# A graph layer's last 724 nodes: three closing chunks in place of two, the last one fetched right behind the last store, in whole tiles and PSUM banks of its own

## The chip, the cores and the metric

The program runs on one core of one Trainium2 chip. A core has TensorE (PE in the profile, with PEld for its weight loads), VectorE (DVE), ScalarE (ACT), GpSimd (POOL) and SyncE (SP, which here only issues transfers and loads registers). The metric is the device time of one execution in microseconds; several executions are timed and their median counts. Before the change the median of three runs is 1881.22 us (1880.9 to 1882.45).

## What is computed

One message-passing layer on a graph of 12,500 nodes with 64 features and 212,500 edges with 32 features, then a residual and a layer norm:

```python
msg_in = concat([nodes[row], nodes[col], edge_features])          # row = src, col = dst
messages = relu(msg_in @ mW1 + mb1) @ mW2 + mb2                   # 160 -> 128 -> 64
aggregated = segment_sum(messages, col, num_segments=12500)
upd = relu(concat([nodes, aggregated]) @ uW1 + ub1) @ uW2 + ub2   # 128 -> 128 -> 64
out = layernorm(x + upd)                                          # over the 64 features
```

The edges come sorted by `dst`, so the edges of a node lie together.

## The kernel before

**Groups of edges.** The edges are worked through in 554 groups (`G`) of 384 (`GE`, three tiles of 128; the last group has 148). For each edge of a group POOL fetches the 64 features of its source node by an indirect transfer, one instruction for each tile of 128 edges (`gather`, L193, into a ring `own_rows`). For some of the groups ahead of the last ten, ACT and DVE copy these features one column at a time from a transposed copy of x instead (`fetch`, L666 and L668). DVE writes beside the features a one-hot row of 32 places that tells which of the 32 nodes from the group's first node on the edge ends at (`onehot`, L430).

TensorE treats a group in three parts, each in a later step than the one ahead of it: `turn` (L456) transposes features and one-hot rows into PSUM, and ACT copies them to `own_operands` (L469); `hidden` (L482) multiplies them with weights in which 32 rows are the projected destination nodes (`own_wm`, loaded by SP at L420), and DVE applies the relu (L493); `sums` (L514) multiplies the one-hot rows with the hidden rows, which gives the sums of the hidden rows of 32 nodes and the number of their edges. ACT moves these (L469 or L524), and SP stores 64 rows of 129 numbers, the upper 32 of them zeros, at the group's first node in one of two tables in device memory (`by_node_177` and `by_node_178`, even and odd groups by turns; `store`, L445).

A step of the main loop over k is turn(k), hidden(k-3) and sums(k-6) up to k = 543. In the last ten steps (`SHORT`) it is turn(k), then one or two sums that are outstanding, then one or two hidden. Since all engines run their instructions in the order in which they are written, and a product waits for all that its step needs, TensorE falls behind wherever one of these is late.

**Updates of nodes.** When all edges of a chunk of 512 nodes (`CH`) are done, the chunk is updated. `plan` gives each chunk the first group that lies certainly behind it (`closes`). `step_update(g)` is called once after each sums(g); it starts a chunk `SETTLED` groups after `closes` when no other is under way, and otherwise does one of its twelve steps:

- `found` (L536): SP fetches the chunk's rows of both tables into two SBUF tiles. Their pool, `found_p`, has one buffer for each, and each fetch waits for the stores into its table.
- `counts`, `count_moved` (L546, L556): TensorE adds the two tables' edge numbers and turns them, by products with the identity matrix; ACT moves them out of PSUM.
- `all_sums`, `moved` (L546, L566): the same for the 128 sums, moved by DVE to `agg`.
- `inner`, `relu` (L572 to L574, L579): three products into one PSUM bank, from the sums, the edge numbers and x; ACT applies the relu.
- `outer`, `stats`, `root`, `scaled` (L586, L588, L595, L596, L602, L607, L610): for each tile of the chunk two products (residual and second layer), mean and variance, the root on ACT, the division, and one transfer of the output (L615).

All PSUM results of an update share one bank (`ups`, one buffer, named `u_ps`). The chunk of 512 nodes from 11,776 closes at group 546, so that it starts after sums(548) and its last steps come when all groups are done. The last chunk has 212 nodes, as two tiles of 106; it never closes, and starts when the chunk ahead of it is finished:

```python
while summed < G:
    step((sums, summed))
    summed += 1
    stored()
while now or waiting:
    step_update(G + SETTLED)
```

Of the kernel before, what the change touches and what calls it, by code (L numbers as in the profile page):

```python
# [10 lines left out]
F32 = mybir.dt.float32  # L11
# [9 lines left out]
P = 128  # L21
# [32 lines left out]
SETTLED = 2  # L54
# [80 lines left out]
def ordered(ctx: ExitStack, tc: tile.TileContext, a, own, ok):  # L135
# [393 lines left out]
    def update(base, p, n):  # L529

        rows, q = slice(base, base + p * n), p * n

        def found():
            parts = [found_p.tile([P, 4, ROW], F32, name=f"found{i}") for i in range(2)]
            for t, table in zip(parts, tables):
                nc.sync.dma_start(t[:p, :n], table[rows, :].rearrange("(n p) w -> p n w", p=p))  # L536
            return parts
# [4 lines left out]
        def joined(parts, w, rows_out):  # L542
            ps = ups.tile([H, CH], F32, name="u_ps")[:rows_out]
            for k in range(n):
                for i, t in enumerate(parts):
                    nc.tensor.matmul(ps[:, k * p : (k + 1) * p], t[:p, k, w], ident[:p, :p],  # L546
                                     start=i == 0, stop=i == 1)
            return ps

# [3 lines left out]
        def count_moved(got):  # L553
            parts, ps = got
            count = up.tile([1, CH], F32, name="count")
            nc.scalar.activation(count[:, :q], ps[:, :q], AF.Copy)  # L556
            return parts, count

        def all_sums(got):
            parts, count = got  # L560
            return joined(parts, slice(0, H), H), count

        def moved(got):
            ps, count = got
            agg = up.tile([H, CH], F32, name="agg")
            nc.vector.tensor_copy(agg[:, :q], ps[:, :q])  # L566
            return agg, count

        def inner(moved_to):
            agg, count = moved_to  # L570
            u_ps = ups.tile([H, CH], F32, name="u_ps")
            nc.tensor.matmul(u_ps[:, :q], wc, agg[:, :q], start=True, stop=False)  # L572
            nc.tensor.matmul(u_ps[:, :q], per_edge, count[:, :q], start=False, stop=False)  # L573
            nc.tensor.matmul(u_ps[:, :q], ux, xc[: D + 1, rows], start=False, stop=True)  # L574
            return u_ps

        def relu(u_ps):
            u = up.tile([H, CH], F32, name="u")
            nc.scalar.activation(u[:, :q], u_ps[:, :q], AF.Relu)  # L579
            return u  # L580

        def outer(u):
            y = ups.tile([H, CH], F32, name="u_ps")[:, : 4 * D].rearrange("p (n d) -> p n d", n=4)
            for k in range(n):
                at = k * p
                nc.tensor.matmul(y[:p, k], xc[: D + 1, base + at : base + at + p], same,  # L586
                                 start=True, stop=False)
                nc.tensor.matmul(y[:p, k], u[:, at : at + p], u2, start=False, stop=True)  # L588
            return y

        def stats(y):
            parts = up.tile([P, 4, nc.vector.BN_STATS_DIM], F32, name="stats")
            mv = up.tile([P, 4, nc.vector.BN_AGGR_DIM], F32, name="mv")
            for k in range(n):
                nc.vector.bn_stats(parts[:p, k], y[:p, k])  # L595
                nc.vector.bn_aggr(mv[:p, k], parts[:p, k])  # L596
            return y, mv

        def root(ym):
            y, mv = ym  # L600
            rstd = up.tile([P, 4], F32, name="rstd")
            nc.scalar.activation(rstd[:p, :n], mv[:p, :n, 1], AF.Sqrt, bias=eps[:p])  # L602
            return y, mv, rstd

        def scaled(ymr):
            y, mv, rstd = ymr
            nc.vector.reciprocal(rstd[:p, :n], rstd[:p, :n])  # L607
            o = up.tile([P, 4, D], F32, name="o")
            for k in range(n):
                nc.vector.tensor_scalar(  # L610
                    o[:p, k], y[:p, k], mv[:p, k, 0:1], rstd[:p, k : k + 1],
                    ALU.subtract, ALU.mult,
                )
            queue = nc.scalar if base + q == N else nc.sync
            queue.dma_start(out[rows, :].rearrange("(n p) d -> p n d", p=p), o[:p, :n])  # L615

        return [found, settled, counts, count_moved, all_sums, moved, inner, relu, outer, stats, root, scaled]
# [111 lines left out]
    waiting = [(closes, update(base, p, n)) for base, p, n, closes in PLAN]  # L729
# [466 lines left out]
```

## Time and profile before

| | |
|---|---|
| median of three timed runs | 1881.22 us |
| profiled execution, its own time | 1878.41 us |
| span of that execution on the core | 1876.7 us |
| POOL's last gather begins | 1833.38 us |
| the last group's store is issued | 1842.77 us |
| the last chunk's fetches are issued | 1851.94 and 1852.37 us |
| the output's last transfer is issued | 1871.30 us |

Times in the profile are counted from the start of the span. A row of the timeline has the start, the length, the engine (PEld is a weight load, SPq and ACTq are transfers issued by SP and ACT), the line, the operation, what it writes and reads, the shape, how many instructions are merged into the row, and in brackets the idle time of the engine ahead of it with what ended it. A product of 32-bit numbers shows as two MATMUL instructions, so x16 of a row are eight products. "PEclk" is the share of TensorE's full clock that was granted, and "DMA share" the mean busy share of the 16 transfer engines.

### The profile page before, as it was taken

The page shows a single profiled execution, that of the slowest core. Times are in us where ns is not written, and L with a number is a line of the kernel's source. Part 1 is how long each engine was busy: PE and PEld are TensorE (multiplying, and loading weights), DVE is VectorE, ACT ScalarE, POOL GpSimd, SP SyncE. Part 2 cuts the span into 40 slices and gives each one's busy share as a digit, 9 for nine tenths or more (in the row PEclk, how much of TensorE's full clock was granted, in tenths as well). Part 3 has the DMA queues.
Part 4 walks back from the last instruction along what each step waited for, and adds up shares of the span by engine and source line. Part 5 has one row for each costly group of instructions (what it writes and reads, how often), then busy time and mean ns, then how long its engine had stood idle before and what let it go on. Part 6 is the DMA issues. An engine that isn't in the chain of part 4 may idle for free. (4 is left out here: it accounts for less than half of the span.)

```text
span 1876.7 us, 66058 instructions
## 1 busy us (share of the span) xinstructions
PE 1495.1 (80%) x13157; PEld 1217.2 (65%) x13157; DVE 1362.5 (73%) x14069; ACT 1619.6 (86%) x13169; POOL 1385.6 (74%) x1473
## 2 busy tenths in 40 slices
PE   4777888888788778787787878878878878788785
PEld 4666666676676666666675666767656756666673
DVE  3346888888888887877777778778777777787731
ACT  3368999999999999999999999989999898999830
POOL 7777777777777777777777777777777777777770
PEclk9888999999999999999999989989989899999897
DMA  5544333333333333333333333333332323333330
GB/s 136 130 109 93 62 74 74 64 75 74 64 72 74 65 74 68 63 71 71 63 68 68 65 71 64 69 71 60 72 73 63 71 60 72 70 63 72 71 70 17
DMA packets 195851, 135.48 MB, mean 72 GB/s; under 512 B 61029, under 2 KB 170650, under 8 KB 195434
## 3 DMA queue, kind: packets, MB, share of 16 engines
q1 hardware_dynamic: 147678, 82.58, 19.0%
q0 software_dynamic: 46912, 48.10, 14.4%
q14 instruction: 307, 2.51, 0.5%
q8 instruction: 110, 1.80, 0.4%
q10 hardware_dynamic: 844, 0.48, 0.1%
HBM read 103.03 MB, written 27.95 MB: 70 GB/s over the span
## 5 line engine op out<-in xcount | busy, mean ns | idle before, releaser
L193 POOL DMA_INDIRECT own_rows<-in_x,src_sb x1466 | 1384.8, 945 | 447.9 <-issue 178.6
L668 ACT ACTIVATE own_operands<-own_xc 64x1 f32 x12480 | 1295.1, 189 | 28.4 <-issue 6.7
L666 DVE COPY own_operands<-own_xc 64x1 f32 x12480 | 893.7, 136 | 283.4 <-issue 177.5
L456 PE MATMUL own_ps<-own_ident,own_rows 128*96 128x128 f32 x1661 | 299.2, 292 | 302.6 <-ACT own_operands L668 109.6
L482 PE MATMUL own_pre<-own_wm,own_operands 128*128 128x128 f32 x3322 | 492.4, 288 | 0.0
L514 PE MATMUL own_ps<-own_h,own_rows 128*32 128x128 f32 x3322 | 482.3, 284 | 0.0
L456 PEld LDWEIGHTS own_ps<-own_ident,own_rows 128*96 128x96 f32 x1661 | 171.2, 132 | 424.7 <-ACT own_operands L668 205.4
L482 PEld LDWEIGHTS own_pre<-own_wm,own_operands 128*128 128x128 f32 x3322 | 444.3, 203 | 2.4 <-issue 1.6
L469 ACT ACTIVATE own_operands<-own_ps 96x513 f32<-96x513 f32 (+2 forms) x554 | 321.8, 581 | 129.5 <-PE own_ps L514 108.0
L493 DVE TENSOR_SCALAR own_h<-own_pre 128x384 f32<-128x384 f32 x553 | 300.1, 543 | 172.4 <-PE own_ps L514 134.7
L514 PEld LDWEIGHTS own_ps<-own_h,own_rows 128*32 128x32 f32 x3322 | 336.6, 116 | 6.0 <-issue 0.2
L514 PE MATMUL own_ps<-own_one,own_rows 128*32 128x1 f32 x3322 | 199.1, 175 | 3.2 <-ACT own_operands L469 1.7
L514 PEld LDWEIGHTS own_ps<-own_one,own_rows 128*32 128x32 f32 x3322 | 152.3, 114 | 75.3 <-issue 11.4
L430 DVE TENSOR_TENSOR own_rows<-iota,dlc 128x96 f32<-128x96 f32 x554 | 132.4, 240 | 0.0
L546 PE MATMUL u_ps<-own_ident,found 128*1 128x128 f32 (+2 forms) x784 | 110.6, 298 | 19.8 <-SPq L1155 11.2
L546 PEld LDWEIGHTS u_ps<-own_ident,found 128*1 128x1 f32 (+2 forms) x784 | 80.8, 144 | 39.4 <-issue 16.7
L397 PE MATMUL u_ps<-w1b,own_xc 65*128 65x128 f32 x196 | 34.8, 332 | 39.8 <-DMA own_xc<-in_xT 15.5
L397 PEld LDWEIGHTS u_ps<-w1b,own_xc 65*128 65x128 f32 x196 | 29.5, 230 | 45.6 <-issue 25.4
L400 ACT ACTIVATE t<-u_ps 128x512 f32<-128x512 f32 (+1 forms) x25 | 14.6, 586 | 41.1 <-DMA by_dst<-t 17.6
L586 PE MATMUL u_ps<-same,own_xc 65*128 65x64 f32 (+1 forms) x196 | 39.5, 283 | 1.1 <-ACT u L579 1.1
L588 PE MATMUL u_ps<-u,u 128*128 128x64 f32 (+1 forms) x196 | 38.3, 277 | 0.0
L586 PEld LDWEIGHTS u_ps<-same,own_xc 65*128 65x128 f32 (+1 forms) x196 | 29.9, 192 | 7.1 <-ACT own_operands L668 3.4
(69 smaller groups left out, 328.6 us busy)
## 6 DMA issues: line engine op xcount, KB each, us to landing
own_operands<-in_efT SPq DMA_DIRECT2D x138, 192.0 KB
own_rows<-in_x,src_sb POOLq DMA_INDIRECT x1466
by_node<-own_operands SPq DMA_DIRECT2D x554, 32.2 KB
found<-by_node SPq DMA_DIRECT2D x48, 258.0 KB
own_wm<-by_dst SPq DMA_DIRECT2D x554, 16.0 KB
by_dst<-t SPq DMA_DIRECT2D x24, 256.0 KB
out<-o SPq DMA_DIRECT2D x24, 128.0 KB
own_xc<-in_xT SPq DMA_DIRECT2D x12, 179.2 KB
```

Of the source, the lines that this page charges most:

```text
L193: nc.gpsimd.indirect_dma_start(out=s[:p, j, :D], out_offset=None, in_=x[:, :], in_offset=bass.IndirectOffsetOnAxis(ap=src_sb[:p, g * TG + ...
L397: nc.tensor.matmul(ps[:, j], xc[: D + 1, base + j * P :][:, :P], w1b, start=True, stop=True)
L430: places_by[g] = nc.vector.tensor_tensor(own.s[g % RING][:, :, D:], iota.unsqueeze(1).to_broadcast([P, TG, W]), dlc[:, g * TG : (g + 1) * ...
L456: nc.tensor.transpose(xt[:, j * P : j * P + p], sides[g] if g in sides and j == TG - 1 else s[:p, j, :], ident[:p, :p])
L469: after(nc.scalar.activation(t[r, c : c + n], ps[r, :n], AF.Copy), step))]
L482: nc.tensor.matmul(pre[:p, j, :], t[:, c + j * P : c + j * P + p], wm[g % NW], start=True, stop=True)
L493: relu_by[g] = [nc.vector.tensor_scalar(h, pre, 0.0, None, ALU.max)]
L514: did.append(nc.tensor.matmul(out_ps, s[:p, j, D:], of(j, p), start=j == 0, stop=j == len(sizes) - 1))
L546: nc.tensor.matmul(ps[:, k * p : (k + 1) * p], t[:p, k, w], ident[:p, :p], start=i == 0, stop=i == 1)
L586: nc.tensor.matmul(y[:p, k], xc[: D + 1, base + at : base + at + p], same, start=True, stop=False)
L666: by[engine] = nc.vector.tensor_copy(o, x_at)
L668: by[engine] = nc.scalar.activation(o, x_at, AF.Copy)
```

## The change

The plan has 26 chunks in place of 25: the 512 nodes from 11,776 become two chunks of 256 (from 11,776, closing at group 535, and from 12,032, closing at group 546), and the 212 nodes from 12,288 remain the last chunk. `SETTLED` is 1, so that each chunk starts one group earlier if nothing else is under way.

```diff
-SETTLED = 2
+SETTLED = 1
...
-    for e in [c * CH for c in range(1, N // CH + 1)] + [N]:
-        n = e - b
-        chunks.append((b, *((P, n // P) if n % P == 0 else (n // 2, 2)),
-                       next((g for g in range(G) if least(g) >= e), G)))
+    whole = N // CH * CH
+    for e in [*range(CH, whole, CH), whole - CH // 2, whole, N]:
+        chunks.append((b, e - b, next((g for g in range(G) if least(g) >= e), G)))
```

The last chunk is cut into a whole tile of 128 nodes and one of 84, and its sums are fetched for 256 nodes: the 44 rows behind the last node are set to zero at the start of the program, by four small transfers on SP.

```diff
+        for table in tables:
+            for n in range(N, NP, W):
+                m = min(W, NP - n)
+                nc.sync.dma_start(table[n : n + m, :],
+                                  own.st[0][D + W : D + W + m, GE : GE + ROW])
```

The last chunk's fetches stand right behind the last group's store, ahead of the steps that the chunk from 12,032 has left:

```diff
+    _, (find, *others) = waiting.pop()
+    parts = find()
     while now or waiting:
         step_update(G + SETTLED)
+    for other in others:
+        parts = other(parts)
```

It uses the four PSUM banks of the groups instead of the shared one, has its sums and edge numbers added in one step, and goes out in two transfers, one on ACT's queue and one on SP's. In every chunk `inner` now has x's product first and the sums' product last; in the last chunk x's product stands ahead of the moves.

```diff
+        def bank(i):
+            if final:
+                return (*own.pre, *own.ps)[i][:, :CH]
+            return ups.tile([H, CH], F32, name="u_ps")
...
+        def own_inner(ps):
+            nc.tensor.matmul(ps[:, :q], ux, xc[: D + 1, base : base + q], start=True, stop=False)
+            return ps
...
+        def both(parts):
+            ps = joined(parts, slice(0, H), 0)
+            count = joined(parts, slice(H, ROW), 1)
+            return parts, ps, count, own_inner(bank(2))
+
+        def both_moved(got):
+            parts, ps, count_ps, u_ps = got
+            agg, _ = moved((ps, None))
+            _, count = count_moved((parts, count_ps))
+            return agg, count, u_ps
...
+            if final:
+                for k, (p, queue) in enumerate(zip(sizes, (nc.scalar, nc.sync))):
+                    queue.dma_start(out[nodes[k], :], o[:p, k])
...
+        if final:
+            return [found, both, both_moved, inner, relu, outer, stats, root, scaled]
```

Three places show what moves. The first is SP's queue at the very end, from the store of group 550 on; `found` is a fetch, `out` an output. Before:

```order
L445 DMA by_node_177<-own_operands 64x516
L445 DMA by_node_178<-own_operands 64x516
L445 DMA by_node_177<-own_operands 64x516
L445 DMA by_node_178<-own_operands 64x516
L615 DMA out<-o 128x4x64
L536 DMA found_94544<-by_node_177 106x2x129
L536 DMA found_94545<-by_node_178 106x2x129
```

SP's queue at the same place after the change:

```order
L449 DMA by_node_177<-own_operands 64x516
L449 DMA by_node_178<-own_operands 64x516
L449 DMA by_node_177<-own_operands 64x516
L449 DMA by_node_178<-own_operands 64x516
L555 DMA found_94547<-by_node_177 128x2x129
L555 DMA found_94548<-by_node_178 128x2x129
L656 DMA out<-o 128x2x64
L653 DMA out<-o 84x64
```

The last chunk's fetches moved ahead of the output of the chunk before it, and an output of the last chunk is now on this queue.

The second place is TensorE from the transposition of the last group (the second row below is its tile of 20 edges) to the first product of the update behind it. Before:

```order
L456 MATMUL own_ps<-own_ident,own_rows 96x128
L456 MATMUL own_ps<-own_ident,own_rows 96x20
L514 MATMUL own_ps<-own_one,own_rows 32x1 x3
L514 MATMUL own_ps<-own_h,own_rows 32x128 x3
L546 MATMUL u_ps<-own_ident,found_94408 128x128
...
L482 MATMUL own_pre<-own_wm,own_operands 128x128
L482 MATMUL own_pre<-own_wm,own_operands 20x128
L514 MATMUL own_ps<-own_one,own_rows 32x1 x2
L514 MATMUL own_ps<-own_h,own_rows 32x128 x2
L572 MATMUL u_ps<-agg,wc 128x512
```

TensorE at the same place after the change:

```order
L460 MATMUL own_ps<-own_ident,own_rows 96x128
L460 MATMUL own_ps<-own_ident,own_rows 96x20
L518 MATMUL own_ps<-own_one,own_rows 32x1 x3
L518 MATMUL own_ps<-own_h,own_rows 32x128 x3
L486 MATMUL own_pre<-own_wm,own_operands 128x128
L486 MATMUL own_pre<-own_wm,own_operands 20x128
L518 MATMUL own_ps<-own_one,own_rows 32x1 x2
L518 MATMUL own_ps<-own_h,own_rows 32x128 x2
L566 MATMUL u_ps<-own_ident,found_94472 128x128
L566 MATMUL u_ps<-own_ident,found_94473 128x128
L566 MATMUL u_ps<-own_ident,found_94472 128x128
L566 MATMUL u_ps<-own_ident,found_94473 128x128
```

The eight products that add the sums of 512 nodes stood between the last group's transposition and its hidden rows; now four, for 256 nodes, stand behind the last group's sums.

The third place is TensorE in the first two of the last ten steps (turn, two sums, two hidden). Before:

```order
L456 MATMUL own_ps<-own_ident,own_rows 96x128 x3
L514 MATMUL own_ps<-own_one,own_rows 32x1 x3
L514 MATMUL own_ps<-own_h,own_rows 32x128 x3
L514 MATMUL own_ps<-own_one,own_rows 32x1 x3
L514 MATMUL own_ps<-own_h,own_rows 32x128 x3
L482 MATMUL own_pre<-own_wm,own_operands 128x128 x6
```

TensorE at the same place after the change:

```order
L460 MATMUL own_ps<-own_ident,own_rows 96x128 x3
L518 MATMUL own_ps<-own_one,own_rows 32x1 x3
L518 MATMUL own_ps<-own_h,own_rows 32x128 x3
L518 MATMUL own_ps<-own_one,own_rows 32x1 x3
L518 MATMUL own_ps<-own_h,own_rows 32x128 x3
L566 MATMUL u_ps<-own_ident,found_94229 1x128
L566 MATMUL u_ps<-own_ident,found_94230 1x128
L566 MATMUL u_ps<-own_ident,found_94229 1x128
L566 MATMUL u_ps<-own_ident,found_94230 1x128
L486 MATMUL own_pre<-own_wm,own_operands 128x128 x6
```

The edge numbers of the chunk from 11,776 are added in this step; its sums, its inner and its outer products follow in the next three steps, at the same spot.

More of the change, by code (lines that the diff above doesn't have):

```diff
@@ L527, in sums, with update, reads @@
         return did, [*relu_by[g], *copy_by[g], *([emptied] if emptied else [])], moved
-    def update(base, p, n):
-        rows, q = slice(base, base + p * n), p * n
+    def update(base, q):
+        final = base + q == N
+        n = (q + P - 1) // P
+        sizes = [min(P, q - k * P) for k in range(n)]
+        nodes = [slice(base + k * P, base + k * P + p) for k, p in enumerate(sizes)]
+        columns_of = [slice(k * P, k * P + p) for k, p in enumerate(sizes)]
+        def bank(i):
+            if final:
+                return (*own.pre, *own.ps)[i][:, :CH]
+            return ups.tile([H, CH], F32, name="u_ps")
+        def reads(i):
+            if final:
+                tc.declare_no_dep(i.ins, group="quiet", reason="TensorE's later product is waited for")
         def found():
@@ L560, in all_sums @@
             parts, count = got
-            return joined(parts, slice(0, H), H), count
+            return joined(parts, slice(0, H), 0), count
         def moved(got):
@@ L727, in row_fetch @@
             rows_by.setdefault(g, []).append(i)
-    waiting = [(closes, update(base, p, n)) for base, p, n, closes in PLAN]
+    waiting = [(closes, update(base, q)) for base, q, closes in PLAN]
     now = []
```

66 lines of the change are left out of this document (36 added, 30 removed).

## The prediction, made before the changed kernel was run

> **What bounds the kernel now.** I read the groups of POOL first, then the timeline from the last gather on, then the chain of waits, then windows of half a microsecond around the fetches.
>
> ```profile
> span 1876.7 us, 66058 instructions
> ...
> L193 POOL DMA_INDIRECT own_rows<-in_x,src_sb x1466 | 1384.8, 945 | 447.9 <-issue 178.6 <-DMA own_rows<-in_x,src_sb 132.3 <-ACT own_operands L668 92.3
> ...
> POOL own_rows L193 <- issue: 178.6, 586, 0.3
> POOL own_rows L193 <- DMA own_rows<-in_x,src_sb: 132.3, 434, 0.3
> ...
> 1833.38 0.90 POOL L193 DMA_INDIRECT own_rows<-in_x,src_sb  x1 [0.30 <-DMA own_rows<-in_x,src_sb]
> ```
>
> ACT is busiest by share, but POOL's 1466 gathers take 945 ns each with 447.9/1466 = 0.31 us between them, and no wait is longer than 0.3: 1466 x 1.25 = 1832 us, which is the span up to the last gather's end at 1834.28. POOL never stands still for another engine, so the stretch up to there is POOL's and **only the 42.4 us behind it can move**, unless the change makes POOL wait.
>
> ```profile
> 1838.18 2.05 PE L546 MATMUL u_ps<-own_ident,found 128*128 128x128 f32 x16
> 1840.07 0.71 PE L482 MATMUL own_pre<-own_wm,own_operands 128*128 128x128 f32 x4
> ...
> 1842.77 0.47 SPq L445 DMA_DIRECT2D by_node<-own_operands  x1
> 1851.43 0.40 SPq L615 DMA_DIRECT2D out<-o  x1
> ...
> 1852.37 0.69 SPq L536 DMA_DIRECT2D found<-by_node  x1
> ...
> 1859.91 1.22 PE L546 MATMUL u_ps<-own_ident,found 106*1 106x106 f32 x6 [2.11 <-SPq L1155]
> ...
> 1871.30 0.52 ACTq L615 DMA_DIRECT2D out<-o  x1
> ```
>
> From the last store (1842.77) the tail is: 9.6 us until the last chunk's second fetch is issued, behind the 512-node chunk's output; 7.5 us until it lands (1859.91); 11.4 us of the last chunk's own chain; 5.4 us from the last output to the end of the span.
>
> **Term 1, the last group.** TensorE now adds no sums ahead of the last group's hidden rows: 16 instructions, 1838.18 to 1839.96, go (-1.8). Against it the 256-node chunk from 11,776 now does its products in the last ten steps. By the rows above and below that is 8 of 16 instructions for the sums (0.9), as many for the numbers (0.9), three products of 256 columns at half of 1.05 (1.6) and half of the 16 from 1846.24 on (0.9): 4.3 us more. The second chunk's numbers are half as many (-0.9).
>
> ```profile
> 1804.08 0.51 PE L456 MATMUL own_ps<-own_ident,own_rows 128*96 128x128 f32 x3 [1.37 <-DMA own_rows<-in_x,src_sb]
> ...
> 1826.59 0.51 PE L456 MATMUL own_ps<-own_ident,own_rows 128*96 128x128 f32 x3 [0.47 <-DMA own_rows<-in_x,src_sb]
> ...
> 1830.38 0.50 PE L456 MATMUL own_ps<-own_ident,own_rows 128*96 128x128 f32 x3 [1.45 <-DMA own_rows<-in_x,src_sb]
> ```
>
> In these steps TensorE waits for gathered rows (the first row is where they begin), 0.5 + 1.5 us behind it. A TensorE that is late has no such waits, so they pay for 1.9 of the 4.3. Sum: 4.3 - 0.9 - 1.9 - 1.8 = **-0.3**, between -1.8 (all of the 4.3 hidden) and +1.6 (no wait pays). I take -0.2: the last store at 1842.6. What is queued behind TensorE there is ACT's move and that store, nothing else.
>
> **Term 2, the fetch.** It stands right behind the store. The first fetch waits until TensorE has read the second 256-node chunk's rows, for the buffer is the same: the last sums end 0.4 us ahead of the store's issue, and 8 instructions take 0.9, so about 1843.3. The second waits for the last store's landing.
>
> ```profile
> 1843.50:1844.50 1.00, 1.00 (x3) 0.24 (x3) 0.00 (x0) 0.00 (x0) 0.00 (x0) 1.00 0.14 33
> 1844.50:1845.50 1.00, 1.00 (x2) 0.22 (x2) 0.00 (x0) 0.00 (x0) 0.00 (x0) 1.00 0.00 0
> ...
> 1853.50:1859.30 5.80, 0.51 (x2) 0.12 (x2) 0.00 (x0) 0.00 (x0) 0.00 (x0) 0.50 0.14 39
> ...
> 1826.00:1829.20 3.20, 2.45 (x23) 1.79 (x21) 0.80 (x2) 0.76 (x2) 2.59 (x3) 1.00 0.80 197
> ```
>
> The last two numbers of a window are the DMA share and GB/s. The store issued at 1842.77 is over by 1844.5, 1.7 us: the second fetch is issued at 1844.4. The old fetch of 106 partitions crept at a share of 0.14, two engines of 16, for 5.8 us; the 128-partition fetch of the 512-node chunk ran at 0.80 and 197 GB/s. So 132 KB take 0.7 us in place of 2.9; with 1.3 us from issue to data (the store has none for 0.7 us, and is over after 1.7), it **lands at 1846.4**, within 1845.8 (data 0.7 behind the issue) and 1849.1 (132 KB still at 39 GB/s, 3.4 us). The Trainium skill ("DMA: Bandwidth & Descriptors", section "Why a DMA increments its semaphore by 16 and not by 1") has an HWDGE transfer use the largest number up to 16 that divides the slowest dimension: 2 engines for 106, 16 for 128. The trace agrees with the 2, and by the rule the 1849.1 falls away.
>
> **Term 3, the middle chunk.** On TensorE the second 256 nodes stand ahead of the last chunk's products.
>
> ```profile
> 1841.23 0.67 DVE L566 COPY agg<-u_ps 128x512 f32<-128x512 f32 x1
> 1843.38 1.12 PE L573 MATMUL u_ps<-count,per_edge 1*128 1x512 f32 x2
> 1844.43 1.12 PE L574 MATMUL u_ps<-own_xc,ux 65*128 65x512 f32 x2
> ...
> 1846.24 0.43 PE L586 MATMUL u_ps<-same,own_xc 65*128 65x64 f32 x2 [0.69 <-ACT u L579]
> ...
> 1847.85 0.39 PE L588 MATMUL u_ps<-u,u 128*128 128x64 f32 x2
> ```
>
> Its sums end at 1843.3; the move of 256 columns takes 0.45 (0.67 for 512 here, 0.39 for 212 in the chain below), three products 1.6, ACT's relu 0.45, four of these eight row pairs 0.9: with the handovers 1846.9. That is later than the landing, so the last chunk **starts at 1846.9** and the fetch has 0.5 us to spare.
>
> **Term 4, the last chunk's own chain.** Before:
>
> ```profile
> 1861.17 0.34 ACT count L556
> ...
> 1861.56 2.05 PE u_ps L546 x8
> 1863.64 0.39 DVE agg L566
> 1864.07 1.08 PE u_ps L572 x2
> 1865.14 1.00 PE u_ps L573 x2
> 1866.14 1.02 PE u_ps L574 x2
> 1867.18 0.35 ACT u L579
> ...
> 1869.32 0.24 DVE stats L595
> ...
> 1870.67 0.60 DVE o L610 x2
> ```
>
> TensorE ran at half its clock: 8 instructions in 2.05 us, 16 of the same form in 2.05 at 1838.18. After, at the full clock: sums 0.9, numbers 0.8, three products of 212 columns at 0.5 each, 1.5 (the moves by ACT and DVE lie beside the numbers and x's product; DVE first ends the middle chunk, 2.0 behind 1846.9 as below, its move is there at 1849.4, and the product that needs it comes at 1849.6), relu 0.45, six instead of eight outer instructions 0.8 (the first pair lies beside the relu), then as before 2.0 from `stats` to the output (1869.32 to 1871.30): 6.4. The output is issued at **1853.3**, 18.0 earlier than 1871.30.
>
> **Term 5, the way out.** The span ends 5.4 us behind the last output. That output now leaves by ACT and by SP, both over 16 or nearly 16 engines. But SP used to be long past its last branch.
>
> ```profile
> L1155 SPq EVENT_SEMAPHORE  x8: 17/17/17, 1856.5 to 1874.6; - x8
> L1155 SPq COMPARE_BRANCH  x1: 54/54/54, 1853.7 to 1853.7; - x1
> ```
>
> It branched at 1853.7 and went on at 1856.5, 2.8 us later. Now it issues (0.4), loads its flag (0.6, from the fetch's issue ending at 1853.06 to the branch), stands for 2.8, checks its eight semaphores (some 0.2), and needs what lies between the last of them and the end, 1874.6 to 1876.7 (2.1): 6.1 us. I take +0.8; below, -1.0 if only the faster landing counts, above +1.0.
>
> **Nothing** I charge for the rest. `SETTLED` shifts the updates by one group, and the four transfers of zeros delay SP's first loads by some 2 us (four issues of 0.5): both lie beside POOL, whose gathers run up to 16 groups (60 us) ahead; without that cover the 2 us would stay.
>
> **Sum:** -0.2 from the store, 1842.6 to 1853.3 in place of 1842.8 to 1871.3 (-17.8), +0.8: **-17.2**. The profiled execution took 1878.41 (span 1876.7 and 1.7 around it), 2.8 less than the median of the three runs, 1881.22; I take the difference from the median: 1864.0.
>
> **Rivals.** *The half clock comes back.*
>
> ```profile
> 1770.84 0.85 PE L456 MATMUL own_ps<-own_ident,own_rows 128*96 128x128 f32 x3 [2.40 <-DMA own_rows<-in_x,src_sb]
> ...
> 1804.00:1812.00 8.00, 7.34 (x78) 6.54 (x79) 1.67 (x4) 2.05 (x6) 6.03 (x7) 1.00 0.27 59
> ...
> 1770.00:1777.20 7.20, 6.36 (x38) 4.75 (x39) 3.78 (x41) 5.34 (x45) 5.37 (x6) 0.53 0.41 79
> ...
> 1848.50:1849.00 0.50, 0.00 (x0) 0.00 (x0) 0.43 (x5) 0.00 (x0) 0.00 (x0) 0.68 0.00 0
> ```
>
> A wait of 2.40 us left the granted clock at 0.53 for 7 us, while that of 1.37 ahead of 1804.08 left 1.00; at the tail it fell half a microsecond behind the last product. The new tail has pauses of 0.5 us only, but several, and short products between them. If it falls, the last chunk's products take twice their 3.8 us (0.9 + 0.8 + 1.5 + 0.6): 1867.8. The Trainium skill ("TensorE: Matmul & The Clock Gate", section "What's actually happening") lets the half rate return only after an idle window of about 3.4 us. By that there is no pause for this rival and the time is 1864.0; the trace differs, as 2.40 us sufficed. I give it 0.20.
>
> *The fetch isn't early.* It shares its buffers with the middle chunk. Were it held until that chunk's output, as now, the fetch would go out at about 1849.3 (1846.9, 2.0 from statistics to output, and 0.4 of its issue) instead of 1844.4; it would land at 1851.3, 4.4 later: 1868.4. Against it: the order has only the middle chunk's sums ahead. 0.07.
>
> *More is hidden:* term 1 at -1.8 and a way out of -0.2 instead of +0.8 give 1861.4. 0.08.
>
> *The tail gains, but something else ends last*, with no change of time: 1881. Nothing in the chain speaks for it. 0.04.
>
> *Slower: SP stands at each fetch.*
>
> ```profile
> SPq L536 <- DMA by_node<-own_operands: 24.3, 23, 2.4
> ```
>
> SP waits 1.06 us for each chunk's fetch until a store has landed. If with `SETTLED = 1` each of the 25 fetches in the loop waited for a store more, as long again, the loads of `own_wm` behind it would be late by 25 x 1.06 = 26 us; where POOL's lead of 16 groups is used up, that reaches the end: 1864.0 + 26 = 1890. It decides from 17.2/25 = 0.7 us a chunk. Against it: the fetch follows the newest store in both kernels, and POOL never waits. 0.03.
>
> **How the numbers follow.** The forecast, 1864.0 (1862 to 1866.2 by term 1's and the landing's bounds), has 0.58. To keep 8 in 10 the range takes in the clock's rival, the held fetch and the better case: 1860 to 1869. Faster by over 0.2% (3.8 us, about what a measurement of this kernel can tell from no change) are all but the last two: 0.93; same 0.04, slower 0.03.
>
> **What would show it.** Right: POOL's last gather still near 1833.4; the last store within 1.7 us of 1842.6; the last fetch about 1.8 us behind it; TensorE's last sums following the middle chunk's outer products without a wait; the last outputs near 1853; SP last at the barrier. Wrong: gaps above 0.3 us between gathers; a wait of over 1 us ahead of the last chunk's sums; a granted clock of 0.50 behind 1843; a last store beyond 1844.4.

## The result, and the profile after

| | before | after |
|---|---|---|
| median of six runs each | 1881.55 us (1879.58 to 1882.45) | 1868.09 us (1865.2 to 1869.99) |
| after / before | | 0.9927, 95% interval 0.9914 to 0.994 |
| profiled execution, its own time | 1878.41 | 1866.26 |
| span of that execution | 1876.7 | 1864.5 |

The kernel is 13.5 us faster by the medians (17.2 were predicted) and 12.2 us by the two profiled executions. The groups of the changed kernel have this for POOL (busy time and mean ns of one, then the idle time ahead of them and what ended it):

```profile
core 0 of [0], span 1864.5 us
...
L192 POOL DMA_INDIRECT own_rows<-in_x,src_sb x1466 | 1385.1, 945 | 447.8 <-issue 177.1 <-DMA own_rows<-in_x,src_sb 126.2 <-ACT own_operands L713 97.2
```

Its timeline, in part by engines:

```profile
1800.91 0.85 PE L460 MATMUL own_ps<-own_ident,own_rows 128*96 128x128 f32 x3 [2.23 <-DMA own_rows<-in_x,src_sb]
...
1833.56 0.89 POOL L192 DMA_INDIRECT own_rows<-in_x,src_sb  x1 [0.30 <-issue]
...
1844.79 1.16 PE L566 MATMUL u_ps<-own_ident,found 128*128 128x128 f32 x8
1845.24 0.47 SPq L449 DMA_DIRECT2D by_node<-own_operands  x1
1845.82 1.71 SPq L555 DMA_DIRECT2D found<-by_node  x2
1849.83 2.08 PE L566 MATMUL own_pre<-own_ident,found 128*128 128x128 f32 x16
1852.00 0.38 SPq L656 DMA_DIRECT2D out<-o  x1
1856.55 0.39 ACTq L653 DMA_DIRECT2D out<-o  x1
1856.80 0.39 SPq L653 DMA_DIRECT2D out<-o  x1
```

POOL is as it was: the same 0.31 us between gathers (447.8/1466), and the last begins 0.2 us later. The whole gain lies behind it. SP's fetch (L555) now follows the store directly, the last chunk's sums follow the middle chunk's products with no wait in brackets, and the last output goes out at 1856.80 instead of 1871.30. Of the 14.5 us gained there 2.3 are lost on the way out: 7.7 us to the end of the span, 5.4 before.

| us from the start of the span | predicted | measured |
|---|---|---|
| last store issued | 1842.6 | 1845.24 |
| last chunk's sums begin | 1846.9 | 1849.83 |
| last output issued | 1853.3 | 1856.80 |
| end of the span | 1859.5 | 1864.5 |

So 5.0 us less was gained in this execution than forecast: 2.6 up to the store, 0.3 in the middle chunk, 0.6 in the last chunk's chain (7.0 instead of 6.4) and 1.5 on the way out.

Two views of the changed kernel show where the first and the last of these arise. The windows (length, busy time of PE, PEld, DVE, ACT, POOL, granted clock, DMA share, GB/s):

```profile
1797.07:1800.48 3.41, 1.61 (x18) 1.22 (x17) 2.18 (x9) 0.74 (x2) 2.51 (x3) 1.00 0.53 110
1800.48:1810.72 10.24, 9.24 (x58) 7.08 (x59) 0.72 (x2) 1.62 (x4) 7.80 (x9) 0.50 0.34 77
...
1844.85:1848.27 3.42, 2.90 (x15) 1.79 (x14) 0.42 (x1) 0.27 (x1) 0.00 (x0) 1.00 0.29 48
1848.27:1851.68 3.41, 2.94 (x25) 2.45 (x24) 1.18 (x7) 0.68 (x2) 0.00 (x0) 1.00 0.16 43
```

TensorE had waited 2.23 us for gathered rows (the timeline's first row, the transposition of group 543, the last before the ten short steps), and from 1800.48 to 1810.72, in this step and the first short one, it ran at half clock. From there on it is the bound: no later step waits for rows. In the tail the clock was 1.00 in this execution. SP's instructions at the end of the program, in the list for their line (length of one in ns, first and last start):

```profile
L1204 SPq EVENT_SEMAPHORE  x8: 17/17/17, 1860.5 to 1862.8; - x8
...
L1204 SPq COMPARE_BRANCH  x1: 54/54/54, 1857.8 to 1857.8; - x1
```

And SP's waits behind 1844 (us in all, how many, the longest):

```profile
SPq L1204 <- SPq L1204: 4.4, 2, 2.6
```

SP branches at 1857.8, behind its output, stands 2.6 us, checks five of its eight semaphores, stands a further 1.8 (the other of the two waits) and is the last at the barrier.

### The profile page after: what moved, and what is told of

Same layout as the page of the kernel before. It is cut to its first block, busy times and chain, and to the rows that moved or that the text cites. A ratio compares the mean times of both kernels' runs of the same rounds, so it can differ in the third digit from the quotient of the medians.

```text
span 1864.5 us, 66091 instructions
## 1 busy us (share of the span) xinstructions
PE 1489.1 (80%) x13163; PEld 1213.9 (65%) x13163; DVE 1364.2 (73%) x14073; ACT 1619.0 (87%) x13172; POOL 1385.9 (74%) x1473
## 5 line engine op out<-in xcount | busy, mean ns | idle before, releaser
L192 POOL DMA_INDIRECT own_rows<-in_x,src_sb x1466 | 1385.1, 945 | 447.8 <-issue 177.1
L566 PE MATMUL u_ps<-own_ident,found 128*1 128x128 f32 (+1 forms) x768 | 103.4, 289 | 9.0 <-DMA found<-by_node 9.0
L566 PEld LDWEIGHTS u_ps<-own_ident,found 128*1 128x1 f32 (+1 forms) x768 | 76.7, 141 | 26.6 <-issue 7.5
L401 PE MATMUL u_ps<-w1b,own_xc 65*128 65x128 f32 x196 | 37.9, 353 | 36.3 <-DMA own_xc<-in_xT 17.2
L622 PE MATMUL u_ps<-same,own_xc 65*128 65x64 f32 x192 | 38.3, 281 | 0.5 <-ACT u L616 0.5
L623 PE MATMUL u_ps<-u,u 128*128 128x64 f32 x192 | 37.1, 275 | 0.0
L622 PEld LDWEIGHTS u_ps<-same,own_xc 65*128 65x128 f32 x192 | 29.0, 190 | 5.6 <-ACT own_operands L713 3.2
```

Of the source, the lines that this page charges most:

```text
L192: nc.gpsimd.indirect_dma_start(out=s[:p, j, :D], out_offset=None, in_=x[:, :], in_offset=bass.IndirectOffsetOnAxis(ap=src_sb[:p, g * TG + ...
L401: nc.tensor.matmul(ps[:, j], xc[: D + 1, base + j * P :][:, :P], w1b, start=True, stop=True)
L566: nc.tensor.matmul(ps[:, k * P : (k + 1) * P], t[:, k, w], ident, start=j == 0, stop=j == 1)
L622: nc.tensor.matmul(y[:p, k], xc[: D + 1, nodes[k]], same, start=True, stop=False)
```

## The experiments

All times below are compared with runs of the kernel before on the same chip. "Behind the gather" counts from the start of POOL's last gather in the same execution, since that varies by 2 us. An experiment's line numbers differ from the changed kernel's by up to 6.

### The changed kernel again, and parts of it undone

No edit; then one for each run:

```diff
 e2 and e4:
-                for k, (p, queue) in enumerate(zip(sizes, (nc.scalar, nc.sync))):
+                for k, (p, queue) in enumerate(zip(sizes, (nc.scalar, nc.scalar))):
 e3 and e4:
-    for e in [*range(CH, whole, CH), whole - CH // 2, whole, N]:
+    for e in [*range(CH, whole, CH), whole, N]:
```

> The changed kernel itself, once more, as the yardstick for the runs beside it. In its first profile the last store is issued 11.7 us behind the start of POOL's last gather (9.4 before the change), and TensorE ran at half its clock from 1800.5 to 1810.7 at the head of the last ten steps. If the lateness is the work of the added chunk, the 11.7 comes again, within 0.5. If it was the half clock, whose place is not the same in every execution, the store stands 9.4 to 10 us behind the gather where TensorE has its full clock there. The end of the span stands 7.7 us behind the last output; expected again, within 0.5. Time 1866 to 1870.

> Both outputs of the last chunk go by ACT's queue, SP has none. Theory: the way out is long because SP issues an output and only then branches to its end, 2.7 us, and stands a further 1.8 us before it goes on; without the output SP branches behind the middle chunk's output, early enough, and the end comes 5.4 to 6.2 us behind the last output instead of 7.7. The second issue on ACT costs 0.4, so 1.1 to 1.9 us less than the changed kernel. Rival: the end follows the landing of the last output, whoever issues it, or ACT branches just as late as SP did: no gain, up to 0.4 slower.

> The 512 nodes from 11,776 stay one chunk, all else as changed. Theory: the added chunk's products in the last ten steps are what makes the last store late, so it comes back to 9.4 us behind the last gather (11.7 with the split); the 512 nodes' outer products end as before the change, 14.9 us behind the gather, against 16.3 with the split, and the last chunk's sums start there. DVE is busier with four tiles of the chunk ahead and gives back up to 0.8: together 0.6 to 1.4 us less than the changed kernel. Rival, the split shortens the tail: the last chunk starts 1 to 2 us later than with it, because the products behind the last store are twice as many (16 instead of 8 for the sums, three products of 1.05 us each instead of 0.65).

> One chunk of 512 and both outputs on ACT's queue together. If both theories hold, the gains add: 1.7 to 3.3 us less than the changed kernel, near 1865.5. If only one of them holds, the gain is that of the single run within 0.5 us.

| | median of five | ratio to before (1881.17), interval | last store behind the gather | last sums to last output | last output to end |
|---|---|---|---|---|---|
| e1, changed again | 1868.61 | 0.993, 0.9917 to 0.9944 | 10.2 | 8.7 | 7.8 |
| e2, both on ACT | 1866.58 | 0.9919, 0.9905 to 0.9932 | 10.0 | 10.8 | 4.8 |
| e3, 512 as one | 1869.15 | 0.9932, 0.9919 to 0.9946 | 8.7 | 8.6 | 8.1 |
| e4, both edits | 1865.7 | 0.992, 0.9906 to 0.9933 | 8.6 | 7.7 | 4.7 |

**The way out is settled.** With no output of its own SP branches early, beside the last chunk's products, and its stand costs nothing. In e2's list for the same line:

```profile
L1204 SPq EVENT_SEMAPHORE  x8: 17/17/17, 1857.1 to 1865.2; - x8
...
L1204 SPq COMPARE_BRANCH  x1: 54/54/54, 1854.4 to 1854.4; - x1
...
L1204 ACTq COMPARE_BRANCH  x1: 58/58/58, 1863.4 to 1863.4; - x1
...
L1204 ACTq EVENT_SEMAPHORE  x1: 17/17/17, 1866.1 to 1866.1; - x1
```

The end comes 4.8 us behind the last output instead of 7.8, of which the second issue on ACT gives back 0.25. ACT does branch late, as the rival had it, and stands 2.7 us (1863.4 to 1866.1); what goes is what SP did behind that, a second stand of 1.8 us and its checks. So the rival (the landing decides, or ACT branches just as late, and nothing is gained) falls. The medians of e1 and e2 don't separate the two (their intervals overlap); the rows do: 7.7 to 8.4 us in the eight profiles of the changed kernel's variants in which SP has an output, 4.7 to 5.2 in the five in which it has none. A rule of the Trainium skill fits: a taken branch out of the instructions at hand forces a fetch of its target ("Runtime: NRT & Kernel Launch", section "Instruction fetch mechanics"); the stand behind the branch is there in both rows, from 1857.8 to 1860.5 in the changed kernel and from 1854.4 to 1857.1 here, but here the last chunk's products cover it.

**The yardstick was not steady.** e1 is the changed kernel, and its last chunk took 8.7 us instead of 7.0. Its windows:

```profile
1840.91:1844.33 3.42, 2.46 (x24) 1.60 (x23) 0.84 (x3) 0.82 (x3) 0.00 (x0) 1.00 0.08 19
1844.33:1847.74 3.41, 2.89 (x16) 1.84 (x16) 0.42 (x1) 0.27 (x1) 0.00 (x0) 1.00 0.22 46
1847.74:1851.15 3.41, 2.94 (x11) 2.22 (x12) 0.01 (x1) 0.38 (x1) 0.00 (x0) 0.50 0.17 46
1851.15:1854.57 3.42, 3.42 (x16) 2.31 (x15) 1.76 (x9) 0.30 (x1) 0.00 (x0) 0.50 0.08 19
```

The prediction's first rival, the half clock, is there in the tail. It came in e2 and e3 too and not in e4, which is why e3's time (expected 0.6 to 1.4 us below the changed kernel's, 0.5 above it) says nothing of the split. It also comes where no pause explains it. In the second row TensorE is busy for 2.89 of 3.41 us, and the next two stretches run at half clock; in the changed kernel's first profile 2.90 of 3.42 us (1844.85 to 1848.27) are followed by a full one. What may differ is how much the products in the stretch use of TensorE's 128 rows. Both have 1.25 us of light products, over 65 rows (x) and over one row (edge numbers); e1's has besides 0.3 us of products over 20 rows (the last group's last tile) where the other has as much over 128. With each product's time counted by its rows over 128, the stretch of e1 is busy for 0.50 of its time, that of the first profile for 0.58. e3, whose light products are longer, shows it best:

```profile
1840.66:1844.07 3.41, 2.84 (x13) 1.13 (x12) 0.48 (x2) 0.27 (x1) 0.00 (x0) 1.00 0.08 19
1844.07:1847.49 3.42, 2.73 (x4) 0.70 (x4) 0.00 (x0) 0.60 (x1) 0.00 (x0) 0.50 0.36 77
```

2.84 of 3.41 us are busy, by rows 0.33, and the clock falls. The Trainium skill's rule that the prediction cites ("TensorE: Matmul & The Clock Gate", section "What's actually happening": half rate after an idle window) would have kept the clock in e1 and in e3; the measurement decides. The count by rows isn't the whole of it: in e4 a stretch of 0.49 kept the full clock, and in e2 the one ahead of the half clock (1843.05 to 1846.46, busy for 2.53 us) has 0.56.

### The light products made heavy

The closing chunks' products over 1 and 65 rows are run over 128, with rows of zeros:

```diff
+    nc.vector.memset(xc[D:, 11776:N], 0.0)
...
-    ux = const.tile([D + 1, H], F32, name="ux")
-    per_edge = const.tile([1, H], F32, name="per_edge")
+    ux = const.tile([P, H], F32, name="ux")
+    per_edge = const.tile([P, H], F32, name="per_edge")
+    numbers = [const.tile([P, CH], F32, name=f"numbers{i}") for i in range(2)]
+    for t in (ux, per_edge, *numbers):
+        nc.vector.memset(t, 0.0)
...
+        rows, one = (P, P) if base >= 11776 else (D + 1, 1)
...
-            nc.tensor.matmul(ps[:, :q], ux, xc[: D + 1, base : base + q], start=True, stop=False)
+            nc.tensor.matmul(ps[:, :q], ux[:rows], xc[:rows, base : base + q], start=True, stop=False)
...
-            nc.tensor.matmul(u_ps[:, :q], per_edge, count[:, :q], start=False, stop=False)
+            nc.tensor.matmul(u_ps[:, :q], per_edge[:one], count[:one, :q], start=False, stop=False)
...
-                nc.tensor.matmul(y[:p, k], xc[: D + 1, nodes[k]], same, start=True, stop=False)
+                nc.tensor.matmul(y[:p, k], xc[:rows, nodes[k]], same[:rows], start=True, stop=False)
```

`same` is made 128 rows high likewise; the last two chunks' edge numbers go to one tile of `numbers` each. e6 adds the outputs on ACT, e7 the 512 nodes as one chunk. e8 is the changed kernel with this edit alone:

```diff
+FILL = 534
...
-            for j, p in enumerate(tiles_of(g))
+            for j, p in [*enumerate(tiles_of(g))] * (2 if FILL <= g < G - SHORT else 1)
```

> As changed, but in the closing chunks from node 11,776 on the products over 1 and over 65 rows (edge numbers and x) run over 128, the added rows being zeros; no more instructions in the tail, two or three small clearings at the start. Theory: the clock falls to half after a stretch of 3.4 us in which TensorE's busy time, each product counted by its rows of 128, stays below about 0.5; the tail's light products (1 and 65 rows) sink below that in about half of the executions, depending on where the stretches begin, and this costs 2 to 4 us. With 128 rows the tail keeps its full clock to the last products in this profile, the slow ones among the times (1868 to 1871) go, and the median is 1 to 3 us below the changed kernel's 1868.6, near 1866. Rival: rows don't count, only time in which TensorE does nothing; half clock in the tail as often as before, times 1865 to 1871, median within 0.5 of the changed kernel's.

> 128 rows and both outputs on ACT's queue. By the theory on rows the tail's clock stays full, by that on the way out the end comes 4.8 us behind the last output (7.8 with SP); together 2.5 us less than the run with 128 rows alone (3.0 for the way out, 0.5 given back for the second issue on ACT), near 1863.5. Rival: the gain of the output on ACT that the earlier run's median showed (2.0) is all of its clock's luck: within 0.5 of 128 rows alone.

> 128 rows, both outputs on ACT and the 512 nodes as one chunk. In the earlier run without the 128 rows, in an execution whose tail had its full clock, the last chunk's sums began 13.9 us behind the last gather, against 16.2 with the split. If that is what the split costs, this run is 2 us below the one beside it with the split, near 1861.5, with the last store 8.6 to 8.8 us behind the gather. Rival: the earlier start was the clock's alone at the head of the last ten steps; then both are equal within 0.5.

> As changed, but the groups 534 to 543 are transposed twice (three more transposes a step, 0.5 us, into the same place with the same result), so that TensorE waits less for gathered rows ahead of the last ten steps. Theory: in the profiles of the changed kernel a wait of 2.2 us there (busy share 0.43 to 0.47 of a stretch of 3.4 us) puts the first two or three of the last ten steps at half clock, and TensorE doesn't make that up again: with the wait filled the clock stays full and the last store stands 9.7 to 10.0 us behind the gather instead of 10.2 to 11.7; 0.5 to 1.7 us less time. Rival: the store is late by the added chunk's products alone; then it stays, and the transposes add up to 0.5 us.

These four ran on a chip that took 2634.29 us for the kernel before. Medians: e5 2625.83, e6 2624.5, e7 2615.26, e8 2630.21, single runs spread over 18 to 34 us. What bounds the kernel is another thing there, as e5's groups show:

```profile
L192 POOL DMA_INDIRECT own_rows<-in_x,src_sb x1466 | 1383.6, 944 | 1147.8 <-ACT own_operands L478 557.2 <-issue 297.1 <-ACT own_operands L719 258.6
...
L719 ACT ACTIVATE own_operands<-own_xc 64x1 f32 x12480 | 1352.2, 189 | 377.1 <-issue 354.7 <-DVE own_h L502 0.3
```

POOL waits 1147.8 us, mostly for ACT, and ACT stands 377 us between its column copies where it stood 28.5 in e1. The last store stands 64 to 70 us behind the gather, so the four times and the place of the store answer nothing, and e8's question, whether a filled wait at the head of the last ten steps brings the store forward, stays open. What the tails show from the last sums on can be used: in e5, e6 and e7 the last chunk ran at full clock, in e8, with the light products, at half; the way out is 7.7, 5.2, 5.1 and 7.8 us. The other questions were put again, with two more parts undone on top of the 128 rows: e10 issues the last chunk's fetches late, e11 gives it the steps and the shared bank of the other chunks. e9 is e5 and e12 is e7 once more.

```diff
 e10:
     _, (find, *others) = waiting.pop()
-    parts = find()
     while now or waiting:
         step_update(G + SETTLED)
+    parts = find()
 e11 (and bank and reads without their branch for the last chunk):
-            return [found, both, both_moved, inner, relu, outer, stats, root, scaled]
+            return [found, settled, counts, count_moved, all_sums, moved, inner, relu, outer, stats, root, scaled]
```

> The 128 rows alone once more, since the chip of the earlier run took 2634 us for the kernel before. As there: with the theory on rows the tail keeps its full clock up to the last products, the last chunk takes 6.8 us from its first sums to its last output, and the times of 1868 to 1871 go: median near 1866, 1 to 3 us below the changed kernel's 1868.6. Rival, only idle time counts: half clock in the tail as often as before, median within 0.5 of 1868.6.

> 128 rows, and the last chunk's fetches moved back behind the middle chunk's last step, as before the change. Theory: the early fetch carries the largest part of the gain that the new code on its own can have: the fetches go out behind the middle chunk's output, 7 to 7.5 us later than now; they land 2 to 3 us behind that, and the last chunk's sums, which follow the middle chunk's products without a wait now, wait 4 to 5 us. 4 to 5 us more than the run with 128 rows beside it. Besides, a wait of that length may put the last chunk at half clock: up to 7 more. Rival: the fetch is hidden either way, because TensorE is behind; less than 1 us.

> 128 rows, and the last chunk with the steps and the one PSUM bank of the other chunks: numbers, then sums, then the inner products, each behind the move of the one ahead; early fetch, whole tiles and the two output queues stay. Theory: its first product waits until DVE has read the middle chunk's rows out of the shared bank, 2.1 us behind that chunk's outer products, and each step adds a hand-over: 3.5 us more than the run with 128 rows beside it, 2.5 to 5, more if the pauses bring the half clock. Rival: the banks and the joint step don't matter, because DVE frees the bank in time: under 1 us.

> 128 rows, both outputs on ACT's queue and the 512 nodes as one chunk, once more: the candidate for the fastest. If the gains add: way out 4.8 to 5.2 us instead of 7.8 with a second issue of 0.5 on ACT (-2.3), last chunk's start 1 to 2 us earlier: 3 to 4.5 us less than 128 rows alone, near 1862. If one 512-node chunk only pays by its clock's luck: 2 to 2.5 less, near 1864.

| | median | ratio to before (1879.66), interval | last store behind the gather | store to last sums | last sums to last output | to end |
|---|---|---|---|---|---|---|
| e9, 128 rows | 1864.86 (1861.75 to 1866.08) | 0.9918, 0.9905 to 0.9932 | 11.4 | 4.2 | 6.8 | 7.9 |
| e10, late fetch | 1870.51 (1869.04 to 1871.44) | 0.995, 0.9936 to 0.9963 | 10.2 | 9.2 | 8.7 | 7.7 |
| e11, old chain | 1869.15 (1868.11 to 1871.11) | 0.9944, 0.993 to 0.9958 | 9.4 | 17.2 to the last output, together | | 8.4 |
| e12, 128 rows, ACT, 512 | 1861.52 (1860.95 to 1862.96) | 0.9903, 0.9887 to 0.9918 | 9.0 | 4.9 | 7.7 | 4.8 |

**The rows.** In e9 the tail keeps its full clock up to the last product, and no run reaches 1868 (the kernel before took 1.5 us less on this chip than on e1's). Its windows:

```profile
1844.42:1847.83 3.41, 2.87 (x16) 2.03 (x14) 0.42 (x1) 0.27 (x1) 0.00 (x0) 1.00 0.23 48
1847.83:1851.24 3.41, 2.96 (x25) 2.46 (x25) 1.35 (x7) 0.68 (x2) 0.00 (x0) 1.00 0.17 44
1851.24:1855.20 3.96, 2.43 (x15) 1.90 (x14) 1.15 (x8) 0.98 (x3) 0.00 (x0) 1.00 0.09 21
```

The first is e1's stretch again, busy for 2.87 us against 2.89, and this time the clock stays. Over all traces with an early fetch and banks of its own, the last chunk's products met half clock in four of six with the light products (e1, e2, e3, e8; not the first and e4) and in none of five with 128 rows (e5, e6, e7, e9, e12). It is no guarantee: in e7 the chunk ahead of the last one met half clock for 3.4 us, behind a stretch that was busy for 0.72 of its time, by rows 0.63. The expected 1 to 3 us are there by the medians as ratios, 0.9918 against e1's 0.993, but the intervals overlap and e1 ran on another chip, so the times alone don't exclude the rival (within 0.5 us); the clock in the traces speaks against it.

**The early fetch** is worth 5.65 us (1870.51 - 1864.86): in e10 TensorE waits 4.8 us for it, and the pause puts the chunk at half clock.

```profile
1850.90 0.92 SPq L561 DMA_DIRECT2D found<-by_node  x2
...
1853.21 4.04 PE L572 MATMUL own_pre<-own_ident,found 128*128 128x128 f32 x16 [4.82 <-DMA found<-by_node]
```

No run undoes the whole tiles alone, so their share stays open. **Banks of its own and the joint step** are worth 4.3 us (1869.15 - 1864.86), the half clock that comes without them included. In e11 the first product waits for DVE's last reading of the shared bank, the sums wait for the numbers' move, and from 1851.07 on it runs at half clock (the window below the timeline's rows):

```profile
1850.24 1.11 PE L570 MATMUL u_ps<-own_ident,found 128*1 128x128 f32 x8 [2.03 <-DVE o L651]
1851.84 2.08 PE L570 MATMUL u_ps<-own_ident,found 128*128 128x128 f32 x8 [0.49 <-ACT numbers L587]
```

```profile
1851.07:1861.00 9.93, 6.52 (x24) 5.12 (x22) 1.83 (x9) 0.98 (x3) 0.00 (x0) 0.50 0.04 10
```

**The fastest** is e12, 18.1 us below the kernel before and 3.3 below e9, with all four runs within 2 us:

```profile
1843.79 0.47 SPq L454 DMA_DIRECT2D by_node<-own_operands  x1
1844.36 1.71 SPq L561 DMA_DIRECT2D found<-by_node  x2
1848.70 2.08 PE L572 MATMUL own_pre<-own_ident,found 128*128 128x128 f32 x16
1855.90 1.08 ACTq L659 DMA_DIRECT2D out<-o  x2
```

No run shows that the split of the 512 nodes pays. The last sums begin 13.9 us behind the gather in both executions without it that kept the full clock (e4, e12) and 15.6 to 16.3 with it (e9 and the first profile); the last store stands 8.6 to 9.0 behind it in three without, 9.4 to 11.7 in six with it. About 0.9 of that is given back, 7.7 us from the sums to the output in both against 6.8 in e9, part of it the second issue on ACT. But the two with the split are also those with the longest half clock ahead of the store. By the medians the kernel without the split is 0.5 us slower than with it in e3 (against e1) and 0.9 faster in e4 (against e2), and of e12's 3.3 us some 2.8 are the way out. A run that differs by the split alone, at full clock on this chip, wasn't made, so whether it costs anything stays open.

## Why the prediction came out as it did

**The bound and the order: right.** POOL's last gather moved by 0.2 us, nothing ahead of it waits longer, and the fetch goes out 0.6 us behind the last store's issue; the rivals of a stand at each fetch and of a held fetch didn't come. What the held fetch would cost was put at 4.4 us, and e10 gave 5.0 from store to sums (9.2 against 4.2), and half clock besides.

**Term 1, the last store, was mis-sized, and by most.** It was to be -0.2 us, at the most +1.6; measured against the gather it moved from 9.4 to 11.7, +2.3. The step that failed is the charge for the numbers, "as many for the numbers (0.9)". They stand in the first short step, from one transposition to the next in the rows below. Before the change:

```profile
1804.08 0.51 PE L456 MATMUL own_ps<-own_ident,own_rows 128*96 128x128 f32 x3 [1.37 <-DMA own_rows<-in_x,src_sb]
...
1808.41 0.49 PE L456 MATMUL own_ps<-own_ident,own_rows 128*96 128x128 f32 x3
```

After it:

```profile
1804.71 0.88 PE L460 MATMUL own_ps<-own_ident,own_rows 128*96 128x128 f32 x3
...
1811.93 0.49 PE L460 MATMUL own_ps<-own_ident,own_rows 128*96 128x128 f32 x3
```

In e2, where TensorE had its full clock there:

```profile
1805.08 0.50 PE L460 MATMUL own_ps<-own_ident,own_rows 128*96 128x128 f32 x3 [1.29 <-DMA own_rows<-in_x,src_sb]
...
1808.87 1.28 PE L566 MATMUL u_ps<-own_ident,found 128*1 128x128 f32 x8 [0.83 <-DMA found<-by_node]
...
1811.53 0.49 PE L460 MATMUL own_ps<-own_ident,own_rows 128*96 128x128 f32 x3
```

The step took 4.3 us before and 7.2 after, 2.9 more; it also began 0.5 later against the gather, the step ahead of it having run at half clock. From its end to the last store it is 34.4 us before and 33.3 after: 1.05 less, where the sum's other parts make 1.2 less. So the rest of the term came as forecast, with the claim that a late TensorE has no waits for rows. Of the 2.9 the half clock isn't all: in e2 the step took 6.5 us, 2.1 more than before, at full clock, of which 0.83 is a wait for the added chunk's own fetch, which the sum left out, and 1.2 the numbers. The other 0.8 and the late beginning go with the half clock, and the sum had a full clock there. Where the half clock lasted 0 to 7 us (e2, e10, e11, e1) the store stood 9.4 to 10.2 us behind the gather, 0 to 0.9 more than before the change and within the bounds; where it lasted 10 us (the first profile, e9) 11.4 to 11.7. This is read across executions, and among the four the store doesn't follow the half clock's length (10.0 with none, 9.4 with 3.4 us); e8, which was to show its part by itself, answered nothing.

**Term 2, the fetch: right.** From the store's issue the data was to be there after 3.8 us; the windows of the changed kernel have it over by then.

```profile
1847.10:1848.00 0.90, 0.90 (x4) 0.57 (x4) 0.00 (x0) 0.00 (x0) 0.00 (x0) 1.00 0.78 116
1848.00:1849.00 1.00, 0.53 (x3) 0.12 (x3) 0.00 (x0) 0.38 (x1) 0.00 (x0) 1.00 0.55 157
1849.00:1849.80 0.80, 0.80 (x8) 0.80 (x9) 0.00 (x0) 0.00 (x0) 0.00 (x0) 1.00 0.00 0
```

At 116 to 157 GB/s and a share of 0.55 to 0.78 it no longer creeps on two engines of 16.

**Term 3, the middle chunk: right within 0.3 us.** The last sums start the moment the outer products end. **Term 4, the own chain:** 7.0 for 6.4 at full clock, 0.6 too short; 6.8 in e9.

**Term 5, the way out, was mis-sized:** +0.8 predicted, +2.3 measured. That SP issues an output and branches late was seen, with its stand of 2.8; that it stands a second time, 1.8 us between its semaphores, was not in the rows of before that the prediction reads, and was taken for 0.2. e2 shows that the whole 3.0 us hang on SP's output.

**The half clock rival** had 0.20 and a time of 1867.8. It is the common case, in four of the six executions profiled with light products: the median is 1868.09, and the one at full clock in the tail that was timed beside it took 1866.26. With 128 rows the same short pauses left the last chunk its full clock in five of five profiles; what the working overlooked is that products over few rows seem to count for little. That the median comes within 0.3 us of the rival's 1867.8 is luck: in e1 the half clock cost 1.2 us in the middle chunk (5.8 from the store to the last sums, 4.6 in the first profile) and 1.7 in the last, not 3.8, and the late store and the way out, which the rival's sum didn't have, make up the rest. So the forecast erred in two terms and the clock, all with one sign, and the range held because it had been widened for the rivals.

**Its own signs.** The gather, the fetch, the last sums without a wait and SP last at the barrier came as named. Of its signs of being wrong two came: a last store beyond 1844.4 (1845.24) and, in e1, e2 and e3, half clock behind 1843.

## What to carry to other kernels

In a tail where one engine's products are few, look at how many of TensorE's rows they use as well as at the gaps: rows of zeros cost no time in the tail here, and the last chunk kept its clock in five profiles of five. Let the queue whose engine has the longest way to the end behind its branch (here SP) finish its issues early, and put the last outputs on another. Splitting a late chunk shortens what stands behind the last group only by what it adds ahead of it; where TensorE is already the bound there, no run here showed a gain.

## What the runs showed of the hardware

- **Clock by rows.** In the fourteen traces the granted clock changes at multiples of 3.41 us. I took each such stretch at full clock with the busy time of the matmuls in it, and set the clock granted in the next stretch against it: 6,368 stretches. With each product counted by its rows over 128 and a limit of 0.515, 187 fall on the wrong side; by time alone, with its best limit of 0.52, 241. Most hold no light products, and there the two are nearly the same; in the 1,124 that do it is 55 against 87, each with its best limit (0.51 and 0.63). A fit with free weights (178 wrong) gives a product over one row a fifth of the weight of one over 128, and one over 65 rows 0.43. So rows count, but they aren't all that counts.
- **A half clock far from idleness.** A stretch with 1.61 us of work in 3.41 was followed by 10.2 us at 0.50 (the changed kernel at 1797.07).
- **A second stand behind a branch.** 1.8 us between two of SP's semaphores, under which the trace has two transfers of instructions of 8 KB each (at 1860.93 and 1861.08; it doesn't say for which engine). That they are the cause isn't shown.
- **A chip that is 40% slower for this kernel.** 2634.29 us against 1881: ACT and DVE stand between column copies (377 and 668 us in all, 28.5 and 286.5 in e1), while the copies themselves are as long as ever (189 ns). The cause was not looked for.
